# Moving a sequence's output products among the feed-forward tiles, with four eviction buffers and a late last tile

## The chip, the cores and the metric

The kernel runs on one core of one Trainium2 chip. A core has TensorE (PE; its weight loads are shown apart as PEld), VectorE (DVE), ScalarE (ACT), GpSimd (POOL), and SyncE (SP), which here only issues DMAs. They run side by side and wait for each other by semaphores. The metric is the device time of one execution in microseconds (us), given as the median of several runs.

## The reference

One block over x of 2 sequences of 1024 tokens and 512 features: `x + attention(xn) * silu(ffn(xn))`, with xn the layer-normalised x.

```python
xn = _layernorm(x, axis=-1)
s = _L0_attn_ref(xn, w_qkv, b_qkv, w_out, b_out)   # 32 heads of 16, causal, ALiBi
g = _silu(_L0_ffn_ref(xn, w_gate, w_up, w_down))
x = x + s * g

# in _L0_attn_ref, after softmax:
out = jnp.einsum('bhqk,bkhd->bqhd', attn, v).reshape(B, S, D)
return jnp.einsum('bsd,od->bso', out, w_out) + b_out

# _L0_ffn_ref: weights rounded to -1, 0, 1 times one scale, combined by octonion signs
gate = oct_ternary_linear(xp, w_gate)    # 512 -> 1360
up = oct_ternary_linear(xp, w_up)        # 512 -> 1360
h = jax.nn.silu(gate) * up
out = oct_ternary_linear(hp, w_down)     # 1360 -> 512
```

## The kernel before

**Attention.** The work is cut into units: a sequence `b`, a group `g` of four heads and a half `qc` of the 1024 queries. A loop in Python (L1303 to L1310) keeps a model of the engines' times and chooses what TensorE does next: the products for the row maxima, the scores and their exponentials, the products with V, and *side* work, which is sorted by a due position. TensorE always keeps the order in which the program emits its instructions. The other engines keep it too as long as `held` is filled; `held.clear()` (L1312) ends that, and from there the order on ACT, DVE, POOL and SP is chosen by the compiler's scheduler, which may also put later instructions among earlier ones.

The last two units are swapped (L799), so sequence 1 ends with its second half of queries (`qc` 1) and then its first (`qc` 0).

**Output products.** A unit's result goes to `att` in DRAM. `out_items` (L731) makes the work that follows for four token tiles of 128: fetch a tile of `att` into `ot`, turn it by four transposes into the PSUM tile `pot`, copy that on ACT to `oT`, multiply it by `wo_sb` in `pout`, add the bias on DVE into `y`, and store that to `proj` in DRAM. Tiles `ot`, `oT` and `y` have two buffers each. Turning runs one tile ahead of the products. These items are side work: all of sequence 0, and of sequence 1 the half `qc` 1. They may begin only when their fetch has landed by the model's time. The last half, `qc` 0 of sequence 1, is kept in `last_outs`.

**Feed-forward.** 2048 tokens in four blocks `tb` of 512, and 1360 hidden features in 11 tiles `mt`, the last of 80. `split` writes a block's xn as a rounded part and a rest. `expand_in` (L1349) writes the signed weights of a tile to `fw[mt]`, which lives in buffers that attention has left; the gate's on ACT, the up weights' on DVE. The loop over `work` (L1449) does for each tile:

- `gate_up`: 8 matmuls into `pg` and 8 into `pu` (two PSUM buffers in all); ACT makes `sg` (SiLU), DVE makes `h`, ACT and POOL split `h` into the two halves of `hs`
- `down` for the tile two steps before: 8 matmuls into the four accumulators `pd`, one for each 128 tokens (`st`). The last call does the last three tiles at once, accumulator by accumulator (L1467).
- in steps 2 to 5, one set of `last_outs`: the turning that is next and one product

After a block's last tile the four accumulators are evicted (L1419): ACT makes `ga` (SiLU), DVE multiplies by the attention result `s_tiles[st]`, POOL (DVE for the last) adds x, held in `wo_sb`, and SP stores the result to `out`. `ga` shares the two buffers `oT` with `sg`; `y` has two, shared with `h`. `load_rest` (L1429) loads `s_tiles` from `proj` and x over `wo_sb`, in the step of tile 8.

The helper `InOrder` issues for all engines but PE, so most rows of the profile name its line, L69; there the tile names tell what is meant.

Of the kernel before, what the change touches and what calls it, by code (L numbers as in the profile page):

```python
# [10 lines left out]
F32 = mybir.dt.float32  # L11
F32R = mybir.dt.float32r
AF = mybir.ActivationFunctionType
ALU = mybir.AluOpType
# [4 lines left out]
P = 128  # L19
B, S, D = 2, 1024, 512  # L20
NT = B * S
H, HD = 32, 16
NG = H // 4
# [52 lines left out]
def kernel(  # L76
# [21 lines left out]
    act_, dve_, pool_, sp_ = (  # L98
        InOrder(tc, engine, held) for engine in (nc.scalar, nc.vector, nc.gpsimd, nc.sync)
    )  # L100
# [3 lines left out]
    def pe(ins):  # L104

        return tc.keep_in_program_order(ins)
# [9 lines left out]
    wqp = ctx.enter_context(tc.tile_pool(name="wqp", bufs=1))  # L116
# [4 lines left out]
    wk = ctx.enter_context(tc.tile_pool(name="wk", bufs=2))  # L121
# [686 lines left out]
    for u in range(NU):  # L808
        its, t = max_items(*units[u])
# [9 lines left out]
    def add(items, first, last, ok):  # L819
        first, last = max(first, -1), max(last, -1)  # L820
        lo, hi = (at[u] if u >= 0 else int(u * size[1]) for u in (first, last))
        total = sum(it[0] for it in items)
        done = 0
        for it in items:
            side.append((lo + (hi - lo) * done / total, ok, it))
            done += it[0]
# [4 lines left out]
    fetches, fetched, last_outs = {}, {}, []  # L831
    turned_out = [0]

    def unit_of(lst, n):
        return lst[n][0] if n < len(lst) else NU

    for b in range(B):
        for hh in range(2):
            n = 2 * b + hh
            u = 8 * n  # L840
            if n == 0:
                continue
            add(
                v_items(b, hh),
                u - 4,
                u - 1,
                lambda n=n: not weights_left()
                and unit_of(vals, V[0]) >= 8 * (n - 1)
                and (n < 2 or not waits_x()),
            )  # L850
        for gp in range(2 - 2 * b, NP):
            n = b * NP + gp
            u = 4 * n
            add(
                qk_items(b, gp),
                u - 6 if n > 1 else -1,
                u - 3,
                lambda b=b, n=n: n < 2 or fills[0] >= 4 * (2 * n - 2) and (b == 0 or not waits_x()),
            )
        for n, qc in enumerate((0, 1) if b + 1 < B else (1, 0)):  # L860
            u = (b + 1) * 2 * NG + n

            first, last = (u - 1, u) if b + 1 == B else (u + 8 + 4 * n, u + 12 + 4 * n)
            its, fetch = out_items(b, qc)
            fetches[b, NG - 1, qc] = fetch
            add(
                its if (b, n) != (B - 1, 1) else last_outs.extend(its) or [],
                first,
                last,
                lambda k=(b, NG - 1, qc): k in fetched and fetched[k] <= now[0],  # L870
            )
    behind = []

    def weights_left():
        return "weights" not in known

    def waits_x():
        return any(it[2] == "x" or it[2] and it[2][0] == "n" for it in behind)
# [4 lines left out]
    for n in order:  # L883
        if n in seen:
            continue
        k = n
# [441 lines left out]
    halves, downs = {}, {}  # L1328

    def split(tb):  # L1330
        src = xnT[:, :, tb * 512 : (tb + 1) * 512]
        if tb % 2 == 0:
            xh, xl = q_ring[0], q_ring[1]
        else:
            if "odd" not in halves:
                halves["odd"] = (
                    wqp.tile([P, KD, 512], F32R, tag="wqr", name="xh_odd"),
                    vp.tile([P, KD, 512], F32R, tag="v", name="xl_odd"),
                )
            xh, xl = halves["odd"]  # L1340
        pool_.tensor_copy(xh, src)
        dve_.tensor_tensor(xl, src, xh, ALU.subtract)
        halves[tb] = (xh, xl)
# [23 lines left out]
    def gate_up(tb, mt):  # L1367
        fs = min(P, HID - mt * P)
        pg = ps_x.tile([P, 512], F32, tag="x", name=f"pg_{tb}_{mt}")
        pu = ps_x.tile([P, 512], F32, tag="x", name=f"pu_{tb}_{mt}")  # L1370
        for n0, ps in ((0, pg), (4, pu)):
            for kt in range(KD):
                for n, part in enumerate(halves[tb]):
                    pe(
                        nc.tensor.matmul(  # L1375
                            ps[:fs, :],
                            lhsT=fw[mt][:, n0 + kt, 0:fs],
                            rhs=part[:, kt, :],
                            start=(kt == 0 and n == 0),
                            stop=(kt == KD - 1 and n == 1),  # L1380
                        )
                    )
        sg = wk.tile([P, 512], F32, tag="oT", name=f"sg_{tb}_{mt}")
        act_.activation(sg[:fs, :], pg[:fs, :], AF.Silu, scale=scale["g"][:fs, 0:1])
        h = wk.tile([P, 512], F32, tag="y", name=f"h_{tb}_{mt}")
        dve_.scalar_tensor_tensor(
            h[:fs, :], pu[:fs, :], scale["u"][:fs, 0:1], sg[:fs, :], ALU.mult, ALU.mult
        )
        home, tag = (wqp, "wq") if (tb * NM + mt) % 3 == 2 else (stg, "st")
        hs = home.tile([P, 2, 512], F32R, tag=tag, name=f"hs_{tb}_{mt}")  # L1390
        act_.copy(hs[:fs, 0, :], h[:fs, :])
        pool_.tensor_tensor(hs[:fs, 1, :], h[:fs, :], hs[:fs, 0, :], ALU.subtract)
        downs[tb, mt] = hs

    def down(tb, mts):
        if mts[0] == 0:
            homes = [(ps_m, "m")] * 2 if tb % 2 else [(ps_e, "e"), (ps_o, "po")]
            homes += [(ps_e, "e")] * 2
            downs[tb] = [
                home.tile([P, 512], F32, tag=tag, name=f"pd_{tb}_{st}")  # L1400
                for st, (home, tag) in enumerate(homes)
            ]
        hs = [downs.pop((tb, mt)) for mt in mts]
        for st, pd in enumerate(downs[tb]):
            for k, mt in enumerate(mts):
                fs = min(P, HID - mt * P)
                for n in range(2):
                    pe(
                        nc.tensor.matmul(  # L1409
                            pd,  # L1410
                            lhsT=hs[k][:fs, n, st * P : (st + 1) * P],
                            rhs=fw[mt][:fs, 8:12, :].rearrange("p s n -> p (s n)"),
                            start=(mt == 0 and n == 0),
                            stop=(mt == NM - 1 and n == 1),
                        )
                    )
        if mts[-1] < NM - 1:
            return
        for st, pd in enumerate(downs[tb]):  # L1419
            n = tb * 4 + st  # L1420
            ga = wk.tile([P, D], F32, tag="oT", name=f"ga_{n}")
            act_.activation(ga, pd, AF.Silu, scale=scale["d"][:, 0:1])
            y = wk.tile([P, D], F32, tag="y", name=f"y2_{n}")
            dve_.tensor_tensor(y, ga, s_tiles[st], ALU.mult)
            eng = dve_ if st == 3 else pool_
            eng.tensor_tensor(y, y, wo_sb[0][:, st, :], ALU.add)
            sp_.dma_start(out=out[n * P : (n + 1) * P, :], in_=y)

    def load_rest(tb):  # L1429

        s_tiles[:] = [bv_sb, mask] + [
            wk.tile([P, D], F32, tag=tag, name=f"s_{tag}_{tb}", bufs=1) for tag in ("scr", "posb")
        ]
        for st in range(4):
            sp_.dma_start(out=s_tiles[st], in_=proj[tb * 4 + st])
        sp_.dma_start(
            out=wo_sb[0],
            in_=x[tb * 512 : (tb + 1) * 512, :].rearrange("(s p) n -> p s n", p=P),
        )

    s_tiles = []
    split(0)
    for mt in range(2):
        expand_in(mt)
# [3 lines left out]
    work = [(tb, mt) for tb in range(NT // 512) for mt in range(NM)]  # L1448
    for n, (tb, mt) in enumerate(work):  # L1449
        if n + 2 < NM:  # L1450
            expand_in(n + 2)
        if mt == NM - 2 and tb + 1 < NT // 512:
            split(tb + 1)
        if mt == 8:
            load_rest(tb)
        gate_up(tb, mt)
        if 2 <= n < len(work) - 1:
            down(work[n - 2][0], [work[n - 2][1]])
        if n == 1 and (B - 1, NG - 1, 0) not in fetched:
            fetches[B - 1, NG - 1, 0]()  # L1460
        if n >= 2:
            while last_outs:
                _, emit, kind = last_outs.pop(0)
                emit()
                if kind == "out":
                    break
    down(work[-1][0], [mt for _, mt in work[-3:]])  # L1467


# [70 lines left out]
```

## Time and profile before

| | us |
|---|---|
| median of 3 runs | 1145.27 (1144.88 to 1146.23) |
| the profiled execution | 1146.23 |
| its span, first to last instruction | 1144.5 |
| PE busy | 1066.6 (93%) |
| DVE, ACT, POOL busy | 678.3, 506.7, 176.2 |
| mean granted PE clock | 0.975 of full speed |

The span and the groups below come from one profiled execution; it is the longest of the three runs. A timeline row gives the start, the length, the engine, the line, the operation with output and inputs by the program's names, the count, and in brackets how long the engine had stood idle before it and what ended that. Matmuls are pipelined: a row's length holds the drain of its last matmul, and the distance between two starts is what the work takes. The attention part ends at about 839 us of the span, and the last instruction of PE ends at about 1133.

### The profile page before, as it was taken

What the parts mean: (1) busy time and instruction counts of PE and PEld (TensorE: products, weight loads), DVE (VectorE), ACT (ScalarE), POOL (GpSimd) and SP (SyncE); (2) the same over time, 40 slices, a digit from 0 to 9 for tenths busy, and PEclk for the clock granted to TensorE, in tenths of its full rate; (3) what the DMA queues carried; (4) which work ended last, traced back from release to release, by engine and by line L of the source; (5) the groups of instructions that cost most, each with busy time, mean ns of one, the idle gap of its engine ahead of it and who ended that gap; (6) DMA issues with size and microseconds to landing.
All of it is one profiled execution on the core that took longest, in us unless ns stands there. A gap on an engine that the chain in (4) does not pass through costs nothing.

```text
span 1144.5 us, 15617 instructions
## 1 busy us (share of the span) xinstructions
PE 1066.6 (93%) x5562; PEld 702.4 (61%) x5562; DVE 678.3 (59%) x1400; ACT 506.7 (44%) x962; POOL 176.2 (15%) x294
## 2 busy tenths in 40 slices
PE   7889969999998999999999999999879999999995
PEld 5554645675655666556566566565546687878783
DVE  5377786757777687777786877878531122131211
ACT  4122647654653634546536356356662123232321
POOL 6401023000111010100110000010001123242322
PEclk9899968999999999999999999999889999999998
DMA  6976463453745416442645154631041013030200
GB/s 194 204 140 153 108 168 83 59 80 112 145 114 129 72 31 124 130 86 43 138 65 76 66 113 99 137 62 42 17 143 65 33 42 111 1 111 1 77 34 37
DMA packets 73740, 104.24 MB, mean 91 GB/s; under 512 B 26992, under 2 KB 31120, under 8 KB 73664
## 3 DMA queue, kind: packets, MB, share of 16 engines
q1 hardware_dynamic: 66336, 87.48, 34.1%
q10 hardware_dynamic: 3552, 9.78, 2.6%
q0 software_dynamic: 3776, 5.98, 2.1%
q8 instruction: 45, 0.74, 0.3%
q14 instruction: 31, 0.25, 0.1%
HBM read 69.58 MB, written 33.10 MB: 90 GB/s over the span
## 4 chain that ended last, share of the span: by engine, by line
PE 73%; DVE 11%; DMA 5%; ACT 4%; issue 4%; POOL 1%; SPq 0%; ACTq 0%; DVEq 0%; POOLq 0%
PE s L538 13%; PE s L654 12%; PE po L692 11%; PE pg L1375 6%; PE pqk L467 6%; PE pu L1375 6%; PE pd L1409 5%; PE pout L761 4%; DVE mx L69 4%; PE s L673 3%; PE pv L425 3%; DMA q_stack<-mr 2%; DVE s L69 2%; ACT p L69 1%; DVE left L69 1%
## 5 line engine op out<-in xcount | busy, mean ns | idle before, releaser
L69 ACT ACTIVATE p<-s 128x512 f32<-128x512 f32 x576 | 309.9, 600 | 124.6 <-PE s L654 70.0
L538 PE MATMUL s<-k_stack,q_stack 126*128 126x512 f32 (+3 forms) x768 | 279.0, 417 | 24.0 <-DVE mx L69 16.2
L654 PE MATMUL s<-q_stack,k_stack 128*128 128x512 f32 (+3 forms) x768 | 229.0, 367 | 11.3 <-DMA q_stack<-mr 7.7
L69 DVE TENSOR_REDUCE mx<-s 128x1 f32<-128x384 f32 (+3 forms) x352 | 226.3, 643 | 11.7
L69 DVE TENSOR_REDUCE left<-s 128x1 f32<-128x512 f32 x256 | 169.2, 686 | 72.4 <-PE s L538 71.3
L538 PEld LDWEIGHTS s<-k_stack,q_stack 126*128 126x128 f32 x768 | 133.1, 194 | 119.0 <-PE s L538 35.7
L654 PEld LDWEIGHTS s<-q_stack,k_stack 128*128 128x128 f32 x768 | 140.8, 193 | 57.4 <-issue 18.5
L69 DVE TENSOR_TENSOR s<-s,mask 128x128 f32<-128x128 f32 (+2 forms) x352 | 124.2, 353 | 40.3 <-PE s L538 38.6
L692 PE MATMUL po<-p,v 128*32 128x512 f32 (+3 forms) x1536 | 140.5, 494 | 0.2 <-ACT p L69 0.2
L467 PE MATMUL pqk<-xnT,wq 128*128 128x512 f32 x256 | 129.4, 613 | 3.9 <-ACT xnT L69 2.0
L69 DVE SCALAR_TENSOR_TENSOR h<-pu,sc_u,sg 128x512 f32<-128x512 f32 (+1 forms) x44 | 33.0, 751 | 166.8 <-PE pu L1375 154.3
L69 POOL DMA_DIRECT2D q_stack<-mr x64 | 32.0, 505 | 603.3 <-ACT mr L69 603.3
L673 PE MATMUL s<-mask_r,ident_r 128*128 128x256 f32 (+1 forms) x320 | 89.2, 279 | 0.0
L69 POOL TENSOR_TENSOR hs<-h,hs 128x512 fp32r<-128x512 f32 (+1 forms) x44 | 57.5, 1307 | 197.9 <-ACT hs L69 197.8
L692 PEld LDWEIGHTS po<-p,v 128*32 128x32 f32 x1536 | 42.6, 110 | 73.0 <-issue 70.5
L69 ACT ACTIVATE sg<-pg,sc_g 128x512 f32<-128x512 f32 (+1 forms) x44 | 30.2, 687 | 100.5 <-PE pg L1375 95.6
L69 ACT ACTIVATE st<-pqk,bqk_sb 128x512 fp32r<-128x512 f32 x32 | 22.0, 688 | 118.2 <-PE pqk L467 102.3
L425 PE MATMUL pv<-wv,xnT 128*128 128x256 f32 x256 | 68.4, 386 | 1.9 <-DVE v L69 1.5
L467 PEld LDWEIGHTS pqk<-xnT,wq 128*128 128x128 f32 x256 | 48.2, 196 | 32.3 <-issue 22.0
L761 PE MATMUL pout<-wo_sb,oT 128*128 128x512 f32 x128 | 62.0, 606 | 1.4 <-ACT oT L69 1.0
L673 PEld LDWEIGHTS s<-mask_r,ident_r 128*128 128x128 f32 x320 | 60.9, 190 | 2.1
L69 ACT CAST hs<-h 128x512 fp32r<-128x512 f32 (+1 forms) x44 | 27.3, 619 | 75.8 <-DVE h L69 75.8
(143 smaller groups left out, 1100.4 us busy)
## 6 DMA issues: line engine op xcount, KB each, us to landing
sp<-st SPq DMA_DIRECT2D x32, 512.0 KB
k_stack<-sp SPq DMA_DIRECT2D x128, 128.0 KB
q_stack<-sp SPq DMA_DIRECT2D x128, 128.0 KB
wqr<-in_wqk_dram ACTq DMA_DIRECT2D x16, 512.0 KB
xt<-in_x_dram SPq DMA_DIRECT2D x16, 256.0 KB
att<-o SPq DMA_DIRECT2D x32, 128.0 KB
ot<-att SPq DMA_DIRECT2D x16, 256.0 KB
proj<-y SPq DMA_DIRECT2D x16, 256.0 KB
```

The lines of the kernel that those rows point to most:

```text
L69: ins = issue(*args, **kwargs)
L425: nc.tensor.matmul(ps[:, 0:256], lhsT=xnT[:, c, b * S + kt * P : b * S + (kt + 1) * P], rhs=wv_tiles[2 * b + hh][:, c, :], start=(c == 0), ...
L467: nc.tensor.matmul(ps, lhsT=wq_tiles[b, gp][:, kt, which, :], rhs=xnT[:, kt, b * S + c * 512 : b * S + (c + 1) * 512], start=(kt == 0), st ...
L538: nc.tensor.matmul(ps[:, j * n : (j + 1) * n], lhsT=q_of(b, g, qc)[0 : NR - 2, first + j, tl * P : (tl + 1) * P], rhs=k_of(b, g, c)[0 : NR ...
L654: nc.tensor.matmul(ps[:, c0 : c0 + w], lhsT=k_of(b, g, kt // 4)[0:NR, h, kt % 4 * P : (kt % 4 + 1) * P], rhs=q[0:NR, h, 512 - w : 512], st ...
L673: pe(nc.tensor.matmul(out, lhsT=ident_r, rhs=rhs, start=False, stop=True))
L692: nc.tensor.matmul(po[32 * i : 32 * i + 32, 512 - w : 512], lhsT=v[:, kt, h * VC : h * VC + 32], rhs=p[:, i * part + c0 : i * part + c0 + ...
L761: nc.tensor.matmul(ps, lhsT=turned[t][:, c, :], rhs=wo_sb[0][:, c, :], start=(c == 0), stop=(c == KD - 1),)
L1375: nc.tensor.matmul(ps[:fs, :], lhsT=fw[mt][:, n0 + kt, 0:fs], rhs=part[:, kt, :], start=(kt == 0 and n == 0), stop=(kt == KD - 1 and n == 1),)
L1409: nc.tensor.matmul(pd, lhsT=hs[k][:fs, n, st * P : (st + 1) * P], rhs=fw[mt][:fs, 8:12, :].rearrange("p s n -> p (s n)"), start=(mt == 0 a ...
```

## The change

- All output products of sequence 1 (both halves) are kept in `last_outs`. One set goes into each step of the feed-forward loop from step 1 on, until all eight are done, in steps 1 to 8.
- The first fetch of each half is emitted by `fetch_last`: before the first `split`, and after an item of `last_outs` as soon as the half before has been turned.
- `load_rest(0)` comes in the step of tile 9 instead of 8; the other blocks' stay.
- The last three tiles' products are reordered: accumulators 0, 1 and 2 first take two tiles, and the last tile's products come after that, with the two older tiles for accumulator 3 among them.
- The subtraction for `hs` of the very last tile is on DVE instead of POOL.
- A block's third and fourth evictions have buffers of their own: `ga` in a tile of the former V weights (`wv`), `y` in the two buffers `ot`. The add of x is on POOL for accumulators 0 and 2 and on DVE for 1 and 3; before, on POOL for 0, 1 and 2.

```diff
@@ the side work
-                its if (b, n) != (B - 1, 1) else last_outs.extend(its) or [],
+                its if b < B - 1 else last_outs.extend(its) or [],
@@ gate_up
-        pool_.tensor_tensor(hs[:fs, 1, :], h[:fs, :], hs[:fs, 0, :], ALU.subtract)
+        eng = dve_ if (tb, mt) == work[-1] else pool_
+        eng.tensor_tensor(hs[:fs, 1, :], h[:fs, :], hs[:fs, 0, :], ALU.subtract)
@@ down
-        for st, pd in enumerate(downs[tb]):
-            for k, mt in enumerate(mts):
+        steps = [(st, range(len(mts))) for st in range(4)]
+        if len(mts) == 3:
+            a, b = (0, 1), (2,)
+            steps = [(0, a), (1, a), (2, a), (0, b), (1, b), (3, a), (2, b), (3, b)]
+        for st, ks in steps:
+            pd = downs[tb][st]
+            for k in ks:
+                mt = mts[k]
...
+        more = wqp.tile([P, 2, D], F32, tag="wv", name=f"ga_more_{tb}")
         for st, pd in enumerate(downs[tb]):
             n = tb * 4 + st
-            ga = wk.tile([P, D], F32, tag="oT", name=f"ga_{n}")
+            ga = more[:, st - 2, :] if st > 1 else wk.tile([P, D], F32, tag="oT", name=f"ga_{n}")
             act_.activation(ga, pd, AF.Silu, scale=scale["d"][:, 0:1])
-            y = wk.tile([P, D], F32, tag="y", name=f"y2_{n}")
+            y = wk.tile([P, D], F32, tag="ot" if st > 1 else "y", name=f"y2_{n}")
             dve_.tensor_tensor(y, ga, s_tiles[st], ALU.mult)
-            eng = dve_ if st == 3 else pool_
+            eng = dve_ if st % 2 else pool_
             eng.tensor_tensor(y, y, wo_sb[0][:, st, :], ALU.add)
@@ the feed-forward loop
+    def fetch_last():
+        for n, k in enumerate(fetches):
+            if k not in fetched and turned_out[0] == 4 * n:
+                fetches[k]()
+                fetched[k] = 0
+
     s_tiles = []
+    fetch_last()
     split(0)
...
-        if mt == 8:
+        if mt == (8 if tb else 9):
             load_rest(tb)
         gate_up(tb, mt)
         if 2 <= n < len(work) - 1:
             down(work[n - 2][0], [work[n - 2][1]])
-        if n == 1 and (B - 1, NG - 1, 0) not in fetched:
-            fetches[B - 1, NG - 1, 0]()
-        if n >= 2:
-            while last_outs:
+        if n >= 1 and last_outs:
+            while True:
                 _, emit, kind = last_outs.pop(0)
                 emit()
+                fetch_last()
                 if kind == "out":
                     break
```

## The prediction

> **What bounds the kernel now.** I read the page's busy line first, then the timeline of each engine at three places: the passage from attention to the feed-forward tiles, the passage from one 512-token block to the next, and the end.
>
> ```profile
> PE 1066.6 (93%) x5562; PEld 702.4 (61%) x5562; DVE 678.3 (59%) x1400; ACT 506.7 (44%) x962; POOL 176.2 (15%) x294
> ```
>
> PE is the bound: moving its work saves nothing unless it fills time in which PE stands still or runs slowly. The PE timeline (start, length, what, idle before) and one row of the table by stretches (PE, PEld, DVE, ACT, POOL busy, granted clock):
>
> ```profile
> 838.25 0.66 PE L712 MATMUL pt<-ident,posb 128*128 128x128 f32 x4 [0.74 <-ACT posb L69]
> 843.62 1.94 PE L745 MATMUL pot<-ident,ot 128*128 128x128 f32 x8 [4.72 <-DMA ot<-att]
> 855.77 3.70 PE L761 MATMUL pout<-wo_sb,oT 128*128 128x512 f32 x8 [0.73 <-ACT oT L69]
> 866.82 2.39 PE L1375 MATMUL pg<-q_stack,k_stack 128*128 128x512 f32 x8
> 885.01 2.41 PE L1375 MATMUL pg<-q_stack,q_stack 128*128 128x512 f32 x8
> 894.37 2.40 PE L1375 MATMUL pg<-q_stack,k_stack 128*128 128x512 f32 x8
> 839.00:867.00 28.00, 21.57 (x57) 10.39 (x57) 6.13 (x11) 9.10 (x32) 1.89 (x1) 0.88 0.40 133
> ```
>
> Attention's last PE work ends at 838.9. Then PE waits 4.72 us for the fetch of token tile 4 of sequence 1, does five output products one after the other with 0.3 to 0.7 us waits between them, at a mean granted clock of 0.88, and starts the first gate product at 866.82: 27.9 us. Among the feed-forward tiles the same work is dense: with one product set a tile takes 894.37-885.01 = 9.36 us, without one 5.44 (964.43 to 969.87).
>
> At a block's end (first of three):
>
> ```profile
> 957.02 0.69 ACT L69 ACTIVATE sg<-pg,sc_g 128x512 f32<-128x512 f32 x1 [1.62 <-DVE y L69]
> 960.66 0.75 DVE L69 SCALAR_TENSOR_TENSOR h<-pu,sc_u,sg 128x512 f32<-128x512 f32 x1 [0.86 <-ACT sg L69]
> 956.23 0.69 DVE L69 TENSOR_TENSOR y<-ga,s_scr 128x512 f32<-128x512 f32 x1 [1.62 <-DMA out_dram<-y]
> 957.76 0.50 PE L1375 MATMUL pg<-xh_odd,q_stack 128*128 128x512 f32 x1 [0.84 <-ACT sg L69]
> 960.65 0.50 PE L1375 MATMUL pu<-xh_odd,q_stack 128*128 128x512 f32 x1 [0.78 <-ACT sg L69]
> ```
>
> The third eviction waits until the first `y` has been written out, the tile's `sg` waits for that eviction's `ga` buffer, and PE for `sg`, twice. From gate product 951.29 to the second after it (964.43) are 13.14 us, against 2 x 5.44: 2.26 lost. The second boundary (1013.53 to 1026.66) loses 2.25; the third has the same waits.
>
> The end:
>
> ```profile
> 1128.75 4.69 PE L1409 MATMUL pd<-fw,hs 80*128 80x512 f32 x19 [0.87 <-POOL hs L69]
> 1131.53 1.21 DVE L69 TENSOR_TENSOR y<-ga,mask 128x512 f32<-128x512 f32 x1 [0.71 <-ACT ga L69]
> 1134.36 0.69 DVE L69 TENSOR_TENSOR y<-ga,s_scr 128x512 f32<-128x512 f32 x1 [1.62 <-DMA out_dram<-y]
> 1137.04 0.69 DVE L69 TENSOR_TENSOR y<-y,wo_sb 128x512 f32<-128x512 f32 x1
> ```
>
> PE waits 1.04 + 0.87 us for the last tile's `hs`; the evictions then wait for two `y` buffers, and the last add ends at 1137.73.
>
> **The change, part by part.**
>
> *Products.* Removed: the 27.9 us. Four of its five sets (sequence 1, tiles 4 to 7) go to feed-forward tiles; the fifth is sequence 0's last product, which in the side list stood behind them. Each moved set issues 4 transposes and 8 matmuls on PE, one ACT copy (0.59), one DVE add (0.69), one fetch and one store on SP. Priced by the four sets that lie among the tiles now (starts 875.10, 885.01, 894.37, 903.72, 912.64, less 5.44 each): 4.47 + 3.92 + 3.91 + 3.48 = 15.8 us. ACT and DVE are busy about 1.3 and 0.8 us of a 5.44 us tile, which hides the copy and the add; without that cover they would cost 4 x 1.3 = 5.1. The other four sets only move from tiles 2-5 to 5-8. The fifth set costs 3.3 us (two took 6.57 from 860.25 to 866.82). No longer gated, it comes earlier, and PE has 3.6 us idle between 801 and 820 that could hold it: 0 to 3.3, I take 2.2, since a group that fills gaps also delays some score products.
>
> Starting the tiles at 839: the gate products need `fw_0` and block 0's split, both written before then. But ACT is still writing signs for later tiles from 838.09 to 846.34, with `sg` and the 1.28 us table load in the same queue. `sg` would be ready at 840.9; if the signs go around it PE loses 0.3 as at 871.33; if all stand ahead of it, `sg` ends at 846.34 + 1.28 + 0.69 = 848.3 against PE's need at 842.6: 5.7. I take 0.5: the oT copy of 844.74 stood among those sign writes at the moment its transposes were done. SP's fetch goes out at 840.1 and lands at 843.6; the first moved set is due after two tiles, at 847 or later, so its 4.7 us wait is covered. The next pair's fetch is issued three tiles ahead of its use. On SP the moved stores wait for their DVE adds, and the load of x over `wo_sb` now waits for the product of tile 8 instead of tile 5 (issued at 913.23 today); what queues behind it are stores and loads for the first evictions, four tiles (21.8 us) later, so I cost that and `load_rest(0)`, one tile later, at nothing. If it were late, the first block end would wait for it. Sum: 27.9 - 15.8 - 2.2 - 0.5 = **9.4 us** (12.1 with neither the 2.2 nor the 0.5; 7.3 with 3.3 and a start of 1.5, six signs of 0.25 in the way; the 5.7 is rival 1's).
>
> *Four eviction buffers.* The new homes (`wv`, `ot`) cost nothing: their last readers, the V products and the turn in tile 7, are over by then. All four `ga` run at once (they end near 953.2, not 955.4), so `sg` of the next tile follows its gate product. `h` of that tile then needs the first `y` written out (956.1, as before) and stands in DVE's queue behind four multiplies and two adds. What is late next is therefore DVE: with POOL's adds in between I get the last DVE add done at 957.4 to 958.5 and `h` at 958.2 to 959.3, against PE's need of its bank at 958.6. Left over: 0 to 0.7 a boundary, I take 0.35: gain 3 x (2.25 - 0.35) = **5.7 us** (4.6 to 6.8).
>
> *The end.* Twelve matmuls of the two older tiles come before the last tile's products: 12 x 0.2275 = 2.73 us cover the cast (done 1127.33) and the subtraction, which on DVE takes some 0.69 (nearest row; 1.29 on POOL) and is done at 1128.1. Behind it on DVE stands only the first multiply, not due before 1129.5. The 24 matmuls run through from 1125.26 to 1130.7. `ga` then starts at 1128.7, 1129.35, 1130.5, 1131.2. DVE has 4 multiplies and 2 adds, POOL 2 adds. If they did not hinder each other the last add would end at 1133.7, 4.0 earlier. But here is the row that decides:
>
> ```profile
> 848.39 2.29 DVE L69 TENSOR_TENSOR xl_odd<-xnT,xh_odd 128x2048 fp32r<-128x2048 f32 x1 [8.22 <-POOL xh_odd L69]
> 940.50 3.38 DVE L69 TENSOR_TENSOR q_stack<-xnT,q_stack 128x2048 fp32r<-128x2048 f32 x1 [0.88 <-POOL q_stack L69]
> 940.43 1.30 POOL L69 TENSOR_TENSOR hs<-h,hs 80x512 fp32r<-80x512 f32 x1
> ```
>
> The same DVE subtraction takes 1.09 us more when a POOL subtraction has begun just before; the 1.21 of the 1131.53 row ends 0.56 after POOL's add. So POOL's first add holds up DVE's, and its second the last one: 1130.9 to 1132.07 POOL; DVE add, multiply, multiply to 1134.06; POOL to 1135.2; last DVE add 1135.8. Gain **2.0 us** (1.5 if DVE always goes first; 4.0 without hindrance). The Trainium skill, SBUF — State Buffer, section Who interferes with whom, says that a DVE instruction with two SBUF inputs and a GpSimd one that reads SBUF exclude each other, whichever came second waiting for all of the first. By that rule the end is the 1135.8 just worked out, without it 1133.7; no row here shows a POOL instruction held through a whole DVE one.
>
> **Sum.** 9.4 + 5.7 + 2.0 = 17.1. The profiled execution took 1146.23 us (span 1144.5 and 1.7 around it): 1129.1. It lies 0.96 above the median 1145.27, so the median forecast is 1128.2.
>
> **Rivals.**
>
> 1. *ACT's sign writes stand ahead of the first `sg`.* PE then idles 5.7 us at the start. For it: ACT did all of them in a row. It costs 5.2 more than I counted, and the clock: after the 4.72 us idle the stretch ran at 0.88, 0.12 x 28 = 3.4 us. 1128.2 + 8.6 = 1136.8. The Trainium skill, TensorE: Matmul & The Clock Gate (The HAM clock gate), says that an idle window of some 3.4 us halves the clock; the 4.72 us wait and the 0.88 agree. Chance 0.12.
> 2. *The block ends stay as they are*, because `h` still waits for DVE, POOL and `y` writes: 1128.2 + 5.7 = 1133.9. For it: the written-out `y` still gates `h`. Against: today's PE waits name `sg`. 0.10.
> 3. *Slower: fetches exposed on SP.* PE is in order, so a fetch queued on SP behind a store that waits for DVE stops every tile behind it. A fetch takes 3.5 us (840.11 to 843.6); exposed at all eight sets that is 28 us: 1128.2 + 28 = 1156. It decides from the fifth exposed set on (5 x 3.5 > 17.1). Against: the four sets there today show no PE wait on a DMA. 0.08.
> 4. *The early product disturbs the planned score order*, or the gap reappears elsewhere, and the gains cancel: 1145. 0.04.
>
> **How the numbers follow.** Forecast 0.66, its own range 1122.4 (all best bounds: 12.1 + 6.8 + 4.0) to 1131.9 (7.3 + 4.6 + 1.5). About 0.2%, 2.3 us, can be told from no change. Faster: 0.66 + 0.12 + 0.10 = 0.88; same 0.04; slower 0.08. The range takes in rivals 1 and 2: 1122 to 1137.
>
> **What would show it.** Right: no `ot` wait of several us on PE after attention's last transposes, gate products within 1 us of them; eight product sets among tiles 1 to 8; tile starts 5.4 to 6.2 us apart at the block ends; the last add 2 us or more nearer to the last gate product. Wrong: a PE wait on `sg` of over 3 us in the first tiles (rival 1), unchanged `sg` waits at block ends (2), PE waits on `ot` in the tiles (3).

## The result, and the profile after

The changed kernel takes 1130.88 us (median of 4 runs, 1127.83 to 1131.62) against 1145.75 beside it: ratio 0.9861, 95% interval 0.9848 to 0.9874, or 14.9 us less. The forecast was 1128.2 (range 1122 to 1137), 17.1 us less. The profiled execution took 1131.04 us, with a span of 1129.2 (before: 1144.5).

The passage to the feed-forward tiles, on PE's timeline (start, length, what, idle before):

```profile
841.75 0.66 PE L712 MATMUL pt<-ident,posb 128*128 128x128 f32 x4 [0.74 <-ACT posb L69]
842.16 2.09 PE L1375 MATMUL pg<-q_stack,k_stack 128*128 128x512 f32 x8
846.39 2.14 PE L1375 MATMUL pg<-q_stack,k_stack 128*128 128x512 f32 x8 [0.32 <-ACT sg L69]
851.55 3.70 PE L761 MATMUL pout<-wo_sb,oT 128*128 128x512 f32 x8 [0.31 <-ACT oT L69]
854.68 2.41 PE L1375 MATMUL pg<-q_stack,k_stack 128*128 128x512 f32 x8
864.04 2.40 PE L1375 MATMUL pg<-q_stack,q_stack 128*128 128x512 f32 x8
```

The first gate product follows attention's last transposes directly, and no row waits for `ot`. From 842.2 to 867 the granted clock is 1.00 (0.88 in the stretch that was here). A tile with a product set takes 9.36 us, as before (854.68 to 864.04).

The first block end, DVE's rows and then PE's:

```profile
944.07 1.76 DVE L69 TENSOR_TENSOR y<-ga,mask 128x512 f32<-128x512 f32 x1 [1.20 <-POOL hs L69]
946.97 1.78 DVE L69 TENSOR_TENSOR y<-ga_more,s_posb 128x512 f32<-128x512 f32 x1
949.38 0.74 DVE L69 SCALAR_TENSOR_TENSOR h<-pu,sc_u,sg 128x512 f32<-128x512 f32 x1
```

```profile
950.18 0.50 PE L1375 MATMUL pu<-xh_odd,q_stack 128*128 128x512 f32 x1 [0.24 <-DVE h L69]
```

POOL in the same stretch:

```profile
944.01 1.28 POOL L69 TENSOR_TENSOR y<-y,wo_sb 128x512 f32<-128x512 f32 x1
946.52 1.67 POOL L69 TENSOR_TENSOR y<-y,wo_sb 128x512 f32<-128x512 f32 x1 [1.23 <-DVE y L69]
```

No `sg` is late any more; `h` is. It stands behind six eviction operations, two of which take 1.77 instead of 0.69, each begun while a POOL add ran. Before the second multiply DVE also stands idle for 1.20 us, until POOL's subtraction for `hs` is done; that wait was there before, too.

The end: PE, DVE and POOL.

```profile
1111.64 5.67 PE L1417 MATMUL pd<-fw,hs 128*128 128x512 f32 x24
```

```profile
1116.49 0.68 DVE L69 TENSOR_TENSOR y<-ga,mask 128x512 f32<-128x512 f32 x1
1117.20 1.64 DVE L69 TENSOR_TENSOR y<-y,wo_sb 128x512 f32<-128x512 f32 x1
1120.08 1.63 DVE L69 TENSOR_TENSOR y<-y,wo_sb 128x512 f32<-128x512 f32 x1
```

```profile
1116.65 1.65 POOL L69 TENSOR_TENSOR y<-y,wo_sb 128x512 f32<-128x512 f32 x1 [7.46 <-DVE y L69]
1119.53 1.64 POOL L69 TENSOR_TENSOR y<-y,wo_sb 128x512 f32<-128x512 f32 x1 [1.23 <-DVE y L69]
```

The 24 matmuls run through, and the last add is done at 1121.71, 10.07 us after the start of the closing `pd` matmuls at 1111.64 (12.47 before, from 1125.26).

**Where the time went.** One warning first. Up to the transposes `pm` at about 774 us, all kernels here run the same order on PE, and yet those start at 770.3 to 775.0 in 14 profiles. The granted clock may have a share in it: up to there the traces show PE at half clock for 27.3 us in the shortest of the 14 (mean clock 0.98) and for 41.0 us in the longest (0.97); it does not order all of those between, and nothing here tests it. What comes after repeats within some 0.6 us where the edit does not touch it, with one exception (experiment 4). So I compare stages from there on; medians carry the 4.6 us of the part before, and differences of 1 to 2 us between medians prove little. Each stage ends at the start of the row named; us:

| kernel | `pm` to last `pt` | to first `pg` | to tile 10's `pg` | to last `pu` matmul | to span end | sum | median |
|---|---|---|---|---|---|---|---|
| before | 64.66 | 28.57 | 68.01 | 190.20 | 19.42 | 370.9 | 1145.75 |
| changed | 67.45 | 0.41 | 83.88 | 185.37 | 17.82 | 354.9 | 1130.88 |
| changed, again | 67.83 | 0.41 | 83.76 | 185.41 | 17.82 | 355.2 | 1130.77 |
| products alone | 67.54 | 0.41 | 83.77 | 190.16 | 19.45 | 361.3 | 1134.49 |
| buffers alone | 64.31 | 28.55 | 68.02 | 185.11 | 19.33 | 365.3 | 1141.35 |
| late tile alone | 64.44 | 29.64 | 67.99 | 190.17 | 19.14 | 371.4 | 1146.0 |
| before, wait filled | 64.70 | 28.75 | 68.01 | 190.16 | 19.39 | 371.0 | 1145.68 |
| adds on DVE | 67.28 | 0.41 | 83.78 | 183.52 | 12.71 | 347.7 | 1123.49 |
| three adds on POOL | 67.84 | 0.41 | 83.77 | 186.34 | 18.28 | 356.6 | 1130.86 |
| ninth set | 64.88 | 0.41 | 86.73 | 185.79 | 17.82 | 355.6 | 1131.05 |
| last block on DVE | 67.79 | 0.41 | 83.78 | 185.39 | 12.71 | 350.1 | 1127.02 |
| blocks 0 to 2 on DVE | 67.26 | 0.41 | 83.78 | 183.52 | 17.81 | 352.8 | 1127.13 |
| tiny POOL copy | 67.34 | 0.41 | 83.80 | 183.52 | 17.68 | 352.8 | 1127.89 |
| DVE and ninth set | 64.65 | 0.41 | 86.73 | 183.93 | 12.71 | 348.4 | 1121.39 |

From before to changed: +2.79 - 28.16 + 15.87 - 4.83 - 1.60 = -15.9; the part before 774 was 0.7 longer in the changed kernel's profile, which leaves the 15.2 of the spans (1144.45 and 1129.23).

### The profile page after: what moved, and what is told of

It reads as the page before. It is cut to its first block, busy times and chain, and to the rows that moved or that the text cites. A ratio compares the mean times of both kernels' runs of the same rounds, so it can differ in the third digit from the quotient of the medians.

```text
span 1129.2 us, 15583 instructions
## 1 busy us (share of the span) xinstructions
PE 1060.6 (94%) x5562; PEld 700.6 (62%) x5562; DVE 684.5 (61%) x1405; ACT 506.6 (45%) x962; POOL 171.8 (15%) x289
## 5 line engine op out<-in xcount | busy, mean ns | idle before, releaser
L69 ACT CAST hs<-h 128x512 fp32r<-128x512 f32 (+1 forms) x44 | 27.3, 621 | 85.3 <-DVE h L69 85.3
```

Of the source, the lines that this page charges most:

```text
L69: ins = issue(*args, **kwargs)
```

## The experiments

**1. Each part alone.** `e1_products` keeps the evictions, the adds and the order of the last tiles as before:

```diff
-            ga = more[:, st - 2, :] if st > 1 else wk.tile([P, D], F32, tag="oT", name=f"ga_{n}")
+            ga = wk.tile([P, D], F32, tag="oT", name=f"ga_{n}")
...
-            eng = dve_ if st % 2 else pool_
+            eng = dve_ if st == 3 else pool_
```

> Only the products are moved; evictions, adds and the last three tiles as before. Theory (the parts add up, each at its own place): the trace of the changed kernel gives 28.57 us from attention's last transposes to the first gate product before and 0.41 after, attention ending 3.50 later, and 15.87 more from the first gate product to that of tile 10: 28.57 - 0.41 - 3.50 - 15.87 = 8.8 us less, 1137.0. Rival (part of the gain needs the new eviction buffers, since sg, oT and ga share two buffers): under 6 us less, above 1139.8.

Measured 1134.49, beside 1145.96 for the kernel before (ratio 0.9906, 0.9892 to 0.992). By stages the products give 9.5 us, and the block ends (190.16) and the end (19.45) are as before: the rival falls. The median shows 11.5; the rest is not in these stages (in this profile the part before 774 was 1.8 us shorter).

`e2_buffers` has only this:

```diff
+        more = wqp.tile([P, 2, D], F32, tag="wv", name=f"ga_more_{tb}")
...
+            ga = more[:, st - 2, :] if st > 1 else wk.tile([P, D], F32, tag="oT", name=f"ga_{n}")
...
+            y = wk.tile([P, D], F32, tag="ot" if st > 1 else "y", name=f"y2_{n}")
...
+            eng = dve_ if st % 2 else pool_
```

> Only the four eviction buffers, with the adds of accumulators 1 and 3 on DVE; products and last three tiles as before. Theory: 1.6 us less at each of three block ends (4.8) and, at the end, 6.6 us from the first ga to the last add as in the changed kernel instead of 8.4, of which 0.7 are given back because two stores run at once: 4.8 + 1.8 - 0.7 = 5.9 less, 1139.9. Rival (DVE is late instead, so block ends give nothing): 1.1 less, 1144.6.

1141.35 (0.996, 0.9944 to 0.9976), 4.6 less. The block ends give 5.1 (4.8 expected); the end gives 0.1 instead of the 1.1 that I expected. What ends the span there is shown under 3.

`e3_late_tile` has only the reordered last products and the last subtraction on DVE (the two hunks in `gate_up` and `down`).

> Only the reordered products of the last three tiles and the last subtraction on DVE; two eviction buffers. Theory: TensorE ends 2.4 us earlier, but the end is set by the evictions' two y buffers, whose chain starts with the first ga, 0.6 us earlier: 0.6 less, 1145.1. Rival (the end of the matmuls sets the end): 2.4 less, 1143.3.

1146.0 (1.0001, 0.9988 to 1.0013): no gain; its end is 0.3 shorter. The end of the matmuls does not set the end: the rival falls. (Its passage to the first `pg`, which the edit does not touch, took 1.07 longer: see experiment 4.) At the end the late tile alone gives 0.3 and the buffers alone 0.1, both together 1.6: the last evictions must neither start late nor queue for `y`.

**2. Does the fifth set cost its price?** `e6_sixth_set` moves sequence 0's last product among the tiles too, nine sets in all:

```diff
-                its if b < B - 1 else last_outs.extend(its) or [],
+                its if b < B - 1 and qc == 0
+                else its[:-KD] if b < B - 1 and not last_outs.extend(its[-KD:])
+                else last_outs.extend(its) or [],
...
-        if mt == (8 if tb else 9):
+        if mt == (8 if tb else 10):
```

> The changed kernel with sequence 0's last product also kept for the feed-forward loop (first of nine sets, tiles 1 to 9; x is loaded over wo_sb one tile later). Theory (PE time is conserved: in attention that product cost its full 3.5 us and filled no gap): attention ends 3.5 earlier, the tiles take 3.5 longer, no change against the changed kernel within 0.7. Rival (it fills gaps in attention at 801 to 820): attention ends no earlier and the tiles take 3.5 longer, 3.5 more.

1131.05 against 1130.77 for the changed kernel beside it:

> The changed kernel again, beside the next three on the same chip: 1130.9, as measured. What the three differ from it is read against this run.

The stages say it more sharply. Without that set in attention the stretch from `pm` to `pt` takes 64.3 to 64.9 us (six profiles, mean 64.6), with it 67.3 to 67.8 (eight, mean 67.5): 2.9 us. Among the tiles it costs 86.73 - 83.79 = 2.9. It costs the same in both places, so on balance it filled no gap. In the changed kernel it stands here:

```profile
804.06 1.02 PE L761 MATMUL pout<-wo_sb,oT 128*128 128x512 f32 x2
806.37 1.02 PE L761 MATMUL pout<-wo_sb,oT 128*128 128x512 f32 x2
808.81 0.41 PE L538 MATMUL s<-k_stack,q_stack 126*128 126x384 f32 x1 [0.65 <-DVE mx L69]
810.21 0.41 PE L538 MATMUL s<-k_stack,q_stack 126*128 126x384 f32 x1 [0.99 <-DVE mx L69]
```

The score products behind it still wait for DVE's maxima, and most of the idle time stayed (3.3 us from 801 to 820, 3.6 before). The reason that these rows suggest, and no run shows by itself: the scores came later by what the set took, so DVE got them later.

`e11_dve_sixth_set` is the same with all adds on DVE:

> All adds on DVE, and sequence 0's last product kept for the feed-forward tiles too. Theory (that product costs 4.2 us in attention, by the mean over profiles, where the order of the scores is changed around it, and 2.95 among the tiles): 1.2 less than all adds on DVE alone (1123.5), 1122.3. Rival (it costs the same in both places): 1123.5.

1121.39 (0.9786, 0.9768 to 0.9805), the lowest median of all. But my theory of 4.2 against 2.95 falls: that 4.2 came from attention's end as seen in the spans, with the variation before 774 in it. By stages this kernel is 0.7 slower than with the adds on DVE alone.

**3. What sets the end.** `e4_adds_dve` puts all four adds on DVE, `e5_adds_pool` three on POOL as before:

```diff
-            eng = dve_ if st % 2 else pool_
+            eng = dve_
```

```diff
-            eng = dve_ if st % 2 else pool_
+            eng = dve_ if st == 3 else pool_
```

> The changed kernel with all four adds of x on DVE. Theory (a POOL add and a DVE operation with two operands in SBUF shut each other out, so a POOL add takes more DVE time than it saves): at a block end h is done by 949.1 where it ended at 950.1, in time for TensorE, 0.53 less at each of three; at the end eight DVE operations of some 0.62 start to start put the last add at 1120.85 instead of 1121.71, and the last two stores no longer run together, 0.7: 1.6 + 0.9 + 0.7 = 3.1 less than the changed kernel. Rival (POOL takes work off DVE, which is late at a block end): two more adds of 0.65 at each of four block ends, 2.6 more.

> The changed kernel with the adds as before, accumulators 0 to 2 on POOL and 3 on DVE. Theory (mutual exclusion): one more POOL add of 1.3 us in DVE's way at each block end, 0.5 more at each of three and 0.5 at the end: 2 more than the changed kernel. Rival (DVE relieved of an add): 0.65 less at each of four places where DVE is late, up to 2.6 less.

`e5_adds_pool`: 1130.86, not told apart by its median; by stages 1.0 more at the block ends (1.5 expected) and 0.5 more at the end (as expected), so the theory has the sign right. `e4_adds_dve`: 1123.49 (0.980, 0.9782 to 0.9817), 7.3 below the changed kernel where 3.1 was expected. The block ends give 1.9. Not all of that need be POOL's hindrance: in this trace the first add also takes up the 1.20 us in which DVE stood idle, and `h` goes out ahead of the last add; no run separates the three. The end gives 5.1, of which the last add accounts for 0.9 and I had given 0.7 to the stores. So something else ended the span. It is in the rows of the program's closing line (queue, operation, count: shortest/median/longest ns, first to last start). Before the change:

```profile
L1536 POOLq DRAIN  x3: 46/98/8571, 1135.1 to 1144.2; - x3
L1536 SPq DRAIN  x3: 7/7/7, 1140.2 to 1143.9; - x3
```

Changed kernel:

```profile
L1552 POOLq DRAIN  x3: 46/98/8954, 1119.5 to 1129.0; - x3
L1552 SPq DRAIN  x3: 7/7/7, 1124.3 to 1128.7; - x3
L1552 DVEq DRAIN  x2: 19/844/1670, 1120.1 to 1128.7; - x2
```

All adds on DVE:

```profile
L1552 POOLq DRAIN  x3: 46/98/8612, 1105.7 to 1121.7; - x3
L1552 SPq DRAIN  x3: 7/7/7, 1121.2 to 1121.5; - x3
```

In the changed kernel POOL's closing drain starts with its last instruction and ends 7.3 us after that one: 1119.5 + 8.95 = 1128.45, where the instruction itself ended at 1121.17. DVE's ends with its last instruction (1120.1 + 1.67 = 1121.8; the instruction ended at 1121.71). SP has seen the last store landed by 1124.3 and then waits until POOL's drain is over; the span ends 0.8 after the drain. Before the change it was the same: stores landed by 1140.2, drain over at 1135.1 + 8.57 = 1143.7. With no late POOL add, the drain is over at 1105.7 + 8.61 = 1114.3 and the store, at 1121.2, ends the span.

Two runs test that by itself. `e8_last_dve` moves the adds of the last block only, `e9_first_three_dve` of the others only:

```diff
-            eng = dve_ if st % 2 else pool_
+            eng = dve_ if st % 2 or tb == NT // 512 - 1 else pool_
```

```diff
-            eng = dve_ if st % 2 else pool_
+            eng = dve_ if st % 2 or tb < NT // 512 - 1 else pool_
```

> The changed kernel with the adds of x on DVE in the last block only; the three other block ends as in the change. Theory (the span ends when POOL's closing drain is over, which in every run so far ends 7.3 us after POOL's last add): POOL's last instruction is then the subtraction of the second last tile, and the stores end the span, 12.7 us after the last pu matmul as with all adds on DVE, where the changed kernel takes 17.8: 5.1 less than the changed kernel, 1125.6. Rival (only the earlier last add and stores that no longer run together count): 1.6 less, 1129.1.

> The changed kernel with the adds of x on DVE in blocks 0 to 2, and as in the change in the last. Theory: the 0.5 to 0.6 us that TensorE still waits for h at each block end goes: from tile 10 of block 0 to the last pu matmul 183.5 us instead of 185.4, 1.9 less, 1128.8; the end stays. Rival (the end made all of the gain): no change, 1130.7.

`e8_last_dve`: 1127.02, its end 12.71 as the theory has it, block ends unchanged. `e9_first_three_dve`: 1127.13, block ends 183.52, end unchanged. The two medians differ from the theory by 1.4 and 1.7 in opposite directions, and by themselves would split the 7.3 us into 3.7 and 3.6; the stages, one profile each, hit the theory within 0.1. `e10_tiny_pool` gives the kernel with all adds on DVE a late POOL instruction that does next to nothing:

```diff
+            if n == NT // P - 1:
+                tiny = wk.tile([P, 4], F32, tag="rs4", name="tiny")
+                pool_.tensor_copy(tiny, y[:, 0:4])
```

> All adds on DVE, and one POOL copy of four columns after the last add, which nothing needs. Theory (closing drain): the drain ends 7.3 us after that copy, some 0.5 us after the last add, and the span 0.7 later: about 5 more than all adds on DVE (1123.5), 1128.5. Rival (a copy that short lies under the last stores, 2.5 us): no change, 1123.5.

1127.89 (0.9847, 0.983 to 0.9864); the end goes from 12.71 to 17.68, +4.97. POOL's timeline, and its drain:

```profile
1118.04 0.19 POOL L69 COPY tiny<-y 128x4 f32<-128x4 f32 x1 [11.67 <-DVE y L69]
```

```profile
L1555 POOLq DRAIN  x3: 46/98/7484, 1118.0 to 1126.0; - x3
```

A copy of 0.19 us costs 5 us of span. The drain is what ended the kernel before and after the change.

**4. What did the low clock cost?** `e7_wait_filled` is the kernel before, with PE kept busy in the wait for the fetch:

```diff
             turned_out[0] += 1
+            if (b, t) == (1, 4):
+                busy = ps_e.tile([P, 512], F32, tag="e", name="busy")
+                for _ in range(36):
+                    pe(nc.tensor.transpose(busy[:, 0:P], ident, ident))
```

> The kernel before, with 36 extra transposes of the identity into a spare accumulator in the 4.7 us in which TensorE waits for the fetch; they are work that nothing needs. Theory (the idle lowers the granted clock, 0.88 over 28 us, and that is part of the 27.9 us): the stretch runs at full clock and the time falls by 3.4 at most, some 2 to 3.4 us, 1142.4 to 1143.8. Rival (the five sets are slow because each waits for oT and y, not for the clock): no change, 1145.7.

1145.68 (1.0001, 0.999 to 1.0011): nothing, though the granted clock is 1.00 from 843 to 866. The theory falls, and the rival holds. PE's timeline shows why, and DVE's:

```profile
843.09 1.28 PE L749 MATMUL pot<-ident,ot 128*128 128x128 f32 x8 [0.95 <-DMA ot<-att]
848.82 0.66 PE L749 MATMUL pot<-ident,ot 128*128 128x128 f32 x4 [0.73 <-ACT oT L69]
850.83 3.70 PE L765 MATMUL pout<-wo_sb,oT 128*128 128x512 f32 x8 [1.35 <-DVE y L69]
```

```profile
847.88 2.29 DVE L69 TENSOR_TENSOR xl_odd<-xnT,xh_odd 128x2048 fp32r<-128x2048 f32 x1 [8.40 <-POOL xh_odd L69]
```

The first set takes 5.73 us (843.09 to 848.82) instead of 7.18, and then the second waits 1.35 for an add that stands on DVE behind `xl_odd`. That operation waits for POOL, and starts 10.3 us after attention's last transposes (10.1 before), whatever PE has done by then. The clock's 1.4 us lay under that wait.

That holds for the 6.8 us at half clock that the kernel before had here (0.50 granted from 840.6 to 847.4). In the profile of `e3_late_tile` the granted clock is 0.50 from 838.25 to 848.50, the first set takes 8.9 us, and the passage 1.07 us more than before. A longer stretch at half clock can thus reach past the cover; this comes from one trace, and no run tests it.

## Why the prediction was right, and where it was off

**The moved products: 9.4 forecast, 9.5 measured** (28.16 - 15.87 - 2.79). The sum comes out so near because two terms were off in opposite directions. The four sets cost 15.87 (forecast 15.8): rows of the same work in the same place carry over. ACT's writing of signs did not delay the start: it was split around `sg`, and PE lost only the 0.32 of the table load, which it also lost before (forecast 0.5 more; measured none). The fifth set was mis-sized the other way, 2.2 against 2.8 to 2.9: the idle time in front of the waits for DVE was no room for it. It cost in attention what it costs among the tiles (2.9); the upper bound, 3.3, was its time in the old passage, with the waits there.

**The block ends: 5.7 forecast, 4.83 measured.** The new lateness was named, DVE's queue ahead of `h`, and it is 0.6 a boundary where 0.35 was taken (inside the 0 to 0.7). POOL's second add met the fourth multiply (the 946.97 row) and not a gap, and both DVE operations held up by POOL's adds (944.07 and 946.97) delay `h`. With the adds on DVE the stage takes 183.52, 6.7 less than before: all of the 3 x 2.25 is won.

**The end: 2.0 forecast, 1.6 measured, but for the wrong reason; that the sizes are near is luck.** The step that failed is the one that let the last add set the end with a fixed rest behind it. The last add came 2.4 earlier, and the end only 1.6. What ended the span is POOL's last add and its drain: that add starts 8.12 us after the last `pu` matmul instead of 10.10, and takes 1.64 instead of 1.26: 1.98 - 0.38 = 1.60. The closing rows were in the profile of before (8571 ns) and were not used in the working.

**The exclusion of DVE and POOL**, on which the 2.0 rested, held in both orders. The POOL add of 1116.65 takes 1.65 instead of 1.27, begun while a DVE multiply ran until 1117.17; the DVE add of 1117.20, begun while that POOL add ran, takes 1.64 instead of 0.69. The Trainium skill, SBUF — State Buffer, section Who interferes with whom, calls the port pair that the two engines share an exclusive lock, and says that the order of issue decides who waits. These rows agree: the POOL add loses 0.38 to a multiply that ran on for 0.52, the DVE add 0.95 to a POOL add that ran on for 1.10. They also show what no row of the prediction did, POOL as the one held up.

**The clock.** The Trainium skill's page TensorE: Matmul & The Clock Gate (section The HAM clock gate) has the clock halved by an idle window of about 3.4 us; the 0.50 granted from 840.6 to 847.4 before, in and behind a wait of 4.72 us, and the 1.00 with the wait filled, agree. The granted clock alone does not say what it costs, and before the change it cost nothing here (experiment 4). I had counted the 27.9 us as a whole, so the sum did not suffer; only rival 1 had a price for the clock, 3.4 us.

**The sum.** From 774 on, 17.1 was forecast and 15.9 measured; of the difference 0.9 is the block ends and 0.4 the end. The median moved 14.9; the remaining 1.0 lies well within the variation before 774, in code that the change does not touch. Rival 1 (signs ahead of `sg`) and rival 3 (fetches exposed) did not occur: no PE row of the tiles waits for a DMA or for more than 0.32 us on `sg`. Of rival 2 a quarter came true (0.6 of 2.25 left). Rival 4 did not occur: the early product cost its price of 2.9 us, and the gains did not cancel.

## What to carry to other kernels

Work that waits for a transfer belongs among tiles that keep the bounding engine busy; price it at what the same work costs there, and count idle time in front of a wait as room only once a run has shown it. Read the closing rows of every engine before an edit at the end: here POOL's drain ended 7.3 us after its last instruction, so it pays to keep POOL out of the last ten microseconds, even for a copy of four columns. And compare stages from a common point where the part before it varies more than the edit is worth.

The version with all adds on DVE beats both kernels: 1123.49 us, or 1121.39 with the ninth set, which cannot be told apart from it.

## What the runs showed of the hardware

- POOL's closing drain ended 7.3 us after its last compute instruction in all 14 profiles: after an add of 1.26 or 1.64 us, a subtraction of 1.30, a copy of 0.19. DVE's ended within 0.1 us of its last.
- The same instructions up to 774 us took 770.3 to 775.0 us from run to run. The time at half clock in them went from 27.3 us (the shortest) to 41.0 (the longest); what else varies there was not tried.
